# A two-layer graph network on Trainium2: edges in 2 MB loads, gathered rows apart from messages, degrees in PSUM, transposes and node stages a step ahead

## The chip, the cores and the metric

The kernel runs on one core of one Trainium2 chip. The metric is device time in microseconds (us) of that core, as a median of several executions; lower is better. A single execution was also taken by the hardware profiler, and all rows of the profile come from that one. Engines are named as in the profile: PE is TensorE (PEld its weight loads), DVE is VectorE, ACT is ScalarE, POOL is GpSimd and SP is SyncE, which only issues transfers here.

## The reference

There are N = 6250 nodes and E = 106250 edges, sorted by `dst`, with 256 float32 features each. `x` becomes `layernorm(x + L0(x))` and then `layernorm(x + L1(x))`; both layers use the same edges.

```python
# layer 0
msg = relu(x[src] + edge_attr)
agg = segment_sum(msg, dst, num_segments=N)
h = x + (x + agg)
f = bn1(h)
f = gelu(f @ W1.T + b1) @ W2.T + b2
L0 = bn2(h + f)
# layer 1
h = gelu((x[src] + edge_attr) @ W1m + b1m)
agg = segment_sum(h @ W2m + b2m, dst, num_segments=N)
deg = segment_sum(ones((E, 1)), dst, num_segments=N)
u = gelu((agg / maximum(deg, 1)) @ W1u + b1u) @ W2u + b2u
L1 = layernorm(x + u) * gamma + beta
```

## The kernel before, in words

**Work and tiles.** Edges are cut into tiles of 128 rows, and eight tiles make a span (`SPAN`, 1024 edges, V = 104 spans) of two groups of four (`GROUPS`, `G`). Nodes are cut into 25 blocks of 256 (`SB`). Because the edges are sorted, a span touches a short window of nodes, at most some 160. The sum over edges is done by matmuls with one-hot matrices in two stages: `into_slots` (L855) adds each tile's 128 rows into 32 slots, two tiles to the same 32, so a span ends as a 128 x 256 PSUM tile `slotP`; ACT copies it to `sums` (L861); `into_blocks` (L879) spreads the 128 slots over the nodes of their window, into the block's PSUM accumulator `acc`.

**What is done for a span.** POOL gathers the 128 source rows of each tile by an indirect transfer (L772), eight to a span, straight into a ring tile (`RING` = 5 tiles of 128 x 8 x 260). Edge features come in 0.5 MB loads of a group (`load_edges`, L760), three spans ahead (`AHEAD`). ACT lifts two edge tiles into PSUM (`lifted`, L809), DVE adds them to the gathered rows in the ring (`add_to_gathered`, L816), ACT applies Relu or Gelu to a group in place (`activated`, L824), DVE makes the one-hots (`one_hots`, L833; `slot_nodes`, L842; `hot3`, L873).

**Layer 1 uses linearity.** The nodes' part, `x1 @ W1m + b1m`, is computed once for each node at the end of layer 0 and stored as `proj` in DRAM, and this is what layer 1 gathers. The edges' part, `edge @ W1m`, needs transposed edge tiles: PE transposes a pair of tiles into PSUM (`turned`, L785, pool `eaP` with one buffer), ACT copies it to SBUF as `eaT` (L790), PE multiplies (`product`, L798, pool `workP` with four buffers). Half of this is done in layer 0 already: for the first group of every span the product `z` is stored to DRAM (`zst`) and loaded in place of edge features in layer 1; the second group's product is made in layer 1. `W2m` and `W1u` are multiplied into one matrix (`join_weights`) between the layers.

**Degrees.** Column 256 of each ring tile holds ones, so in layer 0 the slot sums also count edges. A one-row matmul for each part of a span (L886) spreads the counts over nodes, DVE adds them up (L890), and each block's degrees go to DRAM (`degd`) and come back in layer 1, broadcast to 128 partitions (`degb`).

**Order.** The program is scheduled by hand: each engine executes its instructions in the order in which the code issues them, and semaphores tie the engines together. `step_0(v)` (L1016) and `step_1(v)` (L1165) are one step each: gathers and, in layer 0, transposes of span v; adds, activations and one-hots of u = v - 1; slot and block sums of w = v - 2. On PE a step of layer 0 is: first transposes of v, slot sums of w, second transposes of v, first product of v, block sums of w, second product of v, and at the end node work. In layer 1 transposes and products are those of u. The node stages of a finished block (`nodes_0` L917 to L987, `nodes_1` L1080 to L1142) are generators; `advance()` runs one part of each at the end of every step. `normalized` (L891 on) is their layernorm, with a square root on ACT (L900).

Of the kernel before, what the change touches and what calls it, by code (L numbers as in the profile page):

```python
# [14 lines left out]
P = 128  # L15
D = 256
# [10 lines left out]
RING = 5  # L27
ROW = 260
AHEAD = 3
# [473 lines left out]
def kernel(  # L503
# [170 lines left out]
    degd = dram.tile([1, N], F32, name="degd")  # L674
    zst = dram.tile([len(window), P, G * D], F32, name="zst")
# [50 lines left out]
    GROUPS = SPAN // G  # L726

    with (
        tc.tile_pool(name="state", bufs=1) as state,
        tc.tile_pool(name="edges", bufs=(AHEAD + 1) * GROUPS) as ep,  # L730
# [4 lines left out]
        tc.tile_pool(name="eaP", bufs=1, space=bass.MemoryType.PSUM) as pse,  # L735
        tc.tile_pool(name="workP", bufs=4, space=bass.MemoryType.PSUM) as psw,
# [11 lines left out]

        ps = work()
# [5 lines left out]
        def load_edges(v, g):  # L755
            counts = tiles_of(v, g)
            ea = ep.tile([P, G, D], F32, name="ea")
            for j, k, n in runs(counts):
                r0 = (v * SPAN + g * G + j) * P
                nc.sync.dma_start(  # L760
                    out=ea[:n, j:k, :],
                    in_=edge_attr[r0 : r0 + (k - j - 1) * P + n, :].rearrange(
                        "(j p) d -> p j d", p=n
                    ),
                )
            return ea

        def gather(v, table):
            for g in range(GROUPS):
                for j, n in enumerate(tiles_of(v, g)):  # L770
                    t = v * SPAN + g * G + j
                    nc.gpsimd.indirect_dma_start(  # L772
                        out=rings[v % RING][:n, g * G + j, :D],
                        out_offset=None,
                        in_=table,
                        in_offset=bass.IndirectOffsetOnAxis(ap=src_sb[:n, t : t + 1], axis=0),
                    )

        def turned(v, g, q, ea):

            pair = tiles_of(v, g)[q : q + 2]
            pe = pse.tile([P, 2, KC, P], F32, name="eaP")
            for j, n in enumerate(pair):
                for k in range(KC):
                    nc.tensor.transpose(  # L785
                        pe[:, j, k, :n], ea[:n, q + j, k * P : (k + 1) * P], ident[:n, :n]
                    )
            eaT = hp.tile([P, 2, KC, P], F32, name="eaT", bufs=3)
            for j, k, n in runs(pair):
                nc.scalar.copy(eaT[:, j:k, :, :n], pe[:, j:k, :, :n])  # L790
            return pair, eaT

        def product(pair, eaT):

            ph = work()
            for j, n in enumerate(pair):
                for k in range(KC):
                    nc.tensor.matmul(  # L798
                        ph[:n, j, :], lhsT=eaT[:, j, k, :n], rhs=w1m_sb[:, k, :],
                        start=(k == 0), stop=(k == KC - 1),  # L800
                    )
            return ph

        def lifted(v, g, q, of):

            pair = tiles_of(v, g)[q : q + 2]
            ps = work()
            for j, k, n in runs(pair):
                nc.scalar.copy(ps[:n, j:k, :], of[:n, q + j : q + k, :])  # L809
            return ps  # L810

        def add_to_gathered(v, g, q, ps):
            at = g * G + q
            r = rings[v % RING]
            for j, k, n in runs(tiles_of(v, g)[q : q + 2]):
                nc.vector.tensor_add(  # L816
                    r[:n, at + j : at + k, :D], ps[:n, j:k, :], r[:n, at + j : at + k, :D]
                )

        def activated(v, g, func):  # L820
            r = rings[v % RING]
            for j, k, n in runs(tiles_of(v, g)):
                at = r[:n, g * G + j : g * G + k, :D]
                nc.scalar.activation(at, at, func)  # L824

        hots, hot2s, sums = {}, {}, {}

        def one_hots(v):

            hots[v] = hp.tile([P, SPAN, SLOTS], F32, name="hot")  # L830
            for j, n in enumerate(tiles_of(v, 0) + tiles_of(v, 1)):
                t = v * SPAN + j
                nc.vector.tensor_scalar(  # L833
                    hots[v][:n, j, :], ramp[:n, :SLOTS], slot[:n, t : t + 1], None,
                    op0=ALU.is_equal,
                )

        def slot_nodes(v):

            lo, hi = window[v]  # L840
            hot2s[v] = hp.tile([P, SB], F32, name="hot2")
            nc.vector.tensor_scalar(  # L842
                hot2s[v][:, : hi - lo], ramp[:, : hi - lo], float(lo), node_of[:, v : v + 1],
                op0=ALU.add, op1=ALU.is_equal,
            )

        def into_slots(v, width):

            counts = tiles_of(v, 0) + tiles_of(v, 1)
            hot, r = hots.pop(v), rings[v % RING]  # L850
            ps = pss.tile([P, D + 1], F32, name="slotP")
            for i in range(PAIR):
                for j in range(i, len(counts), PAIR):
                    n, q = counts[j], j // PAIR
                    nc.tensor.matmul(  # L855
                        ps[q * SLOTS : (q + 1) * SLOTS, :width],
                        lhsT=hot[:n, j, :], rhs=r[:n, j, :width],
                        start=(i == 0), stop=(i == PAIR - 1 or j + 1 == len(counts)),
                    )
            sums[v] = hp.tile([P, D + 1], F32, name="sums")  # L860
            nc.scalar.copy(sums[v][:, :width], ps[:, :width])  # L861

        def into_blocks(v, acc, opened, degs=None):

            its, hot, lo0 = sums.pop(v), hot2s.pop(v), window[v][0]
            for b, lo, hi in parts(v):
                at, fresh = hot[:, lo - lo0 : hi - lo0], b not in acc
                begins = opened(b) if fresh else False
                if begins:

                    lo, hi = b * SB, b * SB + shape(b)[0]
                    at = hp.tile([P, SB], F32, name="hot3")[:, : hi - lo]
                    nc.vector.tensor_scalar(  # L873
                        at, ramp[:, : hi - lo], float(lo), node_of[:, v : v + 1],
                        op0=ALU.add, op1=ALU.is_equal,
                    )
                cols = slice(lo - b * SB, hi - b * SB)
                for k in range(KC):
                    nc.tensor.matmul(  # L879
                        acc[b][:, k, cols], lhsT=its[:, k * P : (k + 1) * P], rhs=at,  # L880
                        start=(begins and k == 0),
                        stop=(last_span[b] == v and k == KC - 1),
                    )
                if degs is not None:
                    ps = work()
                    nc.tensor.matmul(  # L886
                        ps[:1, 0, : hi - lo], lhsT=its[:, D : D + 1], rhs=at,
                        start=True, stop=True,
                    )
                    nc.vector.tensor_add(degs[b][:, cols], degs[b][:, cols], ps[:1, 0, : hi - lo])  # L890
            return [b for b in sorted(acc) if last_span[b] == v]  # L891

        def normalized(tos, of, n, H):

            stats = npool.tile([P, SH, 6], F32, name="stats")
            mv = npool.tile([P, SH, 2], F32, name="mv")
            for h in range(H):
                nc.vector.bn_stats(stats[:n, h, :], of[:n, h, :])
                nc.vector.bn_aggr(mv[:n, h, :], stats[:n, h, :])  # L899
            nc.scalar.activation(mv[:n, :H, 1], mv[:n, :H, 1], AF.Sqrt, bias=eps[:n, :])  # L900
            nc.vector.reciprocal(mv[:n, :H, 1], mv[:n, :H, 1])
            if tos is None:
                return mv
            for h in range(H):
                nc.vector.tensor_scalar(
                    tos[:n, h, :], of[:n, h, :], mv[:n, h, 0:1], mv[:n, h, 1:2],
                    op0=ALU.subtract, op1=ALU.mult,
                )

        running = []  # L910

        def advance():

            for gen in list(running):
                if next(gen, "done") == "done":
                    running.remove(gen)


        def nodes_0(b, acc, xb, deg):
            width, H, n = shape(b)  # L920
# [94 lines left out]
        def step_0(v):  # L1015
            u, w = v - 1, v - 2  # L1016
            if v + AHEAD < V:
                load_0(v + AHEAD)
# [252 lines left out]
```

## Time and profile before

| what | value |
|---|---|
| median of 3 runs | 2815.48 us (2808.16 to 2825.01) |
| the profiled execution | 2831.86 us |
| its span | 2830.0 us |
| granted TensorE clock, mean of the span | 0.889 |
| PE busy | 2125.9 us, 75% |
| PE weight loads busy | 1607.0 us, 57% |
| POOL busy | 1575.0 us, 56% |
| DVE busy | 1430.2 us, 51% |
| ACT busy | 1348.9 us, 48% |
| moved by DMA | 531.79 MB, 188 GB/s on average |

A busy share is a mean over stretches that differ: start (0 to 99.5 us), layer 0 (to 1356.9), the seam between the layers (to 1461.9), layer 1 (to 2791.2) and the tail. A row of the profile names the line, the engine, the operation, what it writes and reads (out<-in with shapes), a count, the busy time with the mean of one, and the idle time of that engine just ahead of these instructions, with what ended it. PEclk is the share of full speed that PE was granted. "issue" as the cause of a wait means that the engine waited for nothing that the profile shows, and "remote" that the releaser isn't on record.

### The profile page before, as it was taken

How to read it: one execution, taken by the hardware profiler on the slowest of the kernel's cores; microseconds unless marked ns; L12 is line 12 of the kernel's file. 1: busy time of each engine (PE TensorE's matmuls, PEld its weight loads, DVE VectorE, ACT ScalarE, POOL GpSimd, SP SyncE). 2: the span in 40 equal slices, each digit the busy share in tenths (PEclk: the TensorE clock that was granted, in tenths of full speed). 3: DMA queues.
4: the chain of work that ended last, by engine and by line, in shares of the span. 5: the costliest groups of instructions: out<-in, count | busy, mean ns of one | idle time of the engine just before them, and what ended most of it. 6: DMA issues, size and time to landing. Idle time of an engine off the chain costs nothing.

```text
span 2830.0 us, 38426 instructions
## 1 busy us (share of the span) xinstructions
PE 2125.9 (75%) x11916; PEld 1607.0 (57%) x11916; DVE 1430.2 (51%) x4130; ACT 1348.9 (48%) x2143; POOL 1575.0 (56%) x1671
## 2 busy tenths in 40 slices
PE   2588888888888888888637777777777777777776
PEld 1465656665665666656425555655555556565554
DVE  3355555555555555556314554455455555454455
ACT  1355555555555555556313444454444444454454
POOL 4666566566566566564266555555556565565550
PEclk8799899899899999899868888988998898898988
DMA  6577677677777777675445555545555554555440
GB/s 197 177 233 222 224 229 224 221 230 227 224 226 220 231 230 232 220 226 177 152 129 178 165 171 181 164 159 182 172 165 183 166 181 156 168 185 169 160 152 11
DMA packets 313740, 531.79 MB, mean 188 GB/s; under 512 B 37989, under 2 KB 233144, under 8 KB 313400
## 3 DMA queue, kind: packets, MB, share of 16 engines
q1 hardware_dynamic: 231190, 307.82, 32.4%
q0 software_dynamic: 79744, 217.71, 26.1%
q10 hardware_dynamic: 2594, 3.71, 0.4%
q8 instruction: 100, 1.64, 0.2%
q14 instruction: 112, 0.92, 0.1%
HBM read 455.34 MB, written 73.75 MB: 187 GB/s over the span
## 4 chain that ended last, share of the span: by engine, by line
PE 50%; issue 18%; DVE 10%; POOL 7%; ACT 6%; another core or an unknown queue 5%; DMA 3%; POOLq 0%; DVEq 0%; SPq 0%; ACTq 0%
PE workP L798 22%; PE slotP L855 8%; POOL ring L772 7%; PE eaP L785 6%; PE acc L879 4%; DVE ring L816 2%; ACT eaT L790 2%; ACT ring L824 1%; PE workP L1125 1%; PE workP L1100 1%; PE workP L979 1%; DMA ring<-proj,src_sb 1%; PE workP L935 1%; PE workP L886 1%
## 5 line engine op out<-in xcount | busy, mean ns | idle before, releaser
L772 POOL DMA_INDIRECT ring<-proj,src_sb x831 | 787.5, 948 | 640.7 <-PE slotP L855 322.8
L772 POOL DMA_INDIRECT ring<-in_x_dram,src_sb x831 | 785.7, 945 | 531.8 <-PE slotP L855 239.0
L798 PE MATMUL workP<-w1m_sb,eaT 128*128 128x256 f32 x3324 | 944.6, 435 | 10.3 <-issue 6.6
L816 DVE TENSOR_TENSOR ring<-workP,ring 128x512 f32<-128x512 f32 x832 | 541.0, 683 | 668.9 <-PE workP L798 148.8
L824 ACT ACTIVATE ring<-ring 128x1024 f32<-128x1024 f32 x418 | 439.5, 1052 | 833.2 <-DVE ring L816 627.6
L798 PEld LDWEIGHTS workP<-w1m_sb,eaT 128*128 128x128 f32 x3324 | 707.5, 223 | 137.0 <-issue 24.8
L855 PE MATMUL slotP<-ring,hot 128*32 128x257 f32 (+1 forms) x3324 | 376.2, 409 | 270.4 <-ACT ring L824 164.1
L785 PE MATMUL eaP<-ident,ea 128*128 128x128 f32 x1662 | 299.1, 309 | 258.8 <-ACT eaT L790 184.6
L785 PEld LDWEIGHTS eaP<-ident,ea 128*128 128x128 f32 x1662 | 213.5, 155 | 386.7 <-ACT eaT L790 261.4
L855 PEld LDWEIGHTS slotP<-ring,hot 128*32 128x32 f32 x3324 | 139.6, 111 | 428.9 <-ACT ring L824 202.3
L790 ACT COPY eaT<-eaP 128x512 f32<-128x512 f32 x416 | 242.1, 582 | 228.4 <-PE slotP L855 119.3
L809 ACT COPY workP<-ea 128x512 f32<-128x512 f32 x624 | 344.9, 589 | 0.0
L879 PE MATMUL acc<-hot,sums 128*128 128x160 f32 (+19 forms) x1360 | 237.0, 303 | 101.5 <-DVE hot L873 62.1
L879 PEld LDWEIGHTS acc<-hot,sums 128*128 128x128 f32 x1360 | 216.5, 205 | 134.2 <-issue 92.1
L833 DVE TENSOR_SCALAR hot<-ramp,slot 128x32 f32<-128x32 f32 x1662 | 268.4, 256 | 0.0
L890 DVE TENSOR_TENSOR degs<-degs,workP 1x160 f32<-1x160 f32 (+24 forms) x170 | 40.3, 243 | 226.3 <-PE slotP L855 97.9
L1032 DVE COPY z<-workP 128x512 f32<-128x512 f32 x104 | 71.7, 689 | 153.6 <-PE workP L798 71.2
L1040 DVE COPY z<-workP 128x512 f32<-128x512 f32 x104 | 71.1, 684 | 148.7 <-PE slotP L855 90.9
L900 ACT ACTIVATE mv<-mv,eps 128x2 f32<-128x2 f32 (+1 forms) x75 | 22.2, 295 | 192.1 <-DVE mv L899 180.0
L1100 PE MATMUL workP<-fT,w 128*128 128x256 f32 (+1 forms) x400 | 94.7, 381 | 0.5 <-DVE fT L1090 0.5
L900 ACT ACT_TABLE_LOAD x73 | 93.7, 1283 | 1.3
L1125 PE MATMUL workP<-w2u_sb,uT 128*128 128x256 f32 (+1 forms) x392 | 89.0, 379 | 3.4 <-ACT uT L1109 3.4
(109 smaller groups left out, 1460.2 us busy)
## 6 DMA issues: line engine op xcount, KB each, us to landing
ea<-in_edge_attr_dram SPq DMA_DIRECT2D x310, 512.0 KB
zst<-z SPq DMA_DIRECT2D x104, 512.0 KB
ea<-zst SPq DMA_DIRECT2D x104, 512.0 KB
ring<-in_x_dram,src_sb POOLq DMA_INDIRECT x831
ring<-proj,src_sb POOLq DMA_INDIRECT x831
xb<-in_x_dram SPq DMA_DIRECT2D x24, 256.0 KB
x1d<-x SPq DMA_DIRECT2D x24, 256.0 KB
proj<-y SPq DMA_DIRECT2D x24, 256.0 KB
```

Of the source, the lines that this page charges most:

```text
L772: nc.gpsimd.indirect_dma_start(out=rings[v % RING][:n, g * G + j, :D], out_offset=None, in_=table, in_offset=bass.IndirectOffsetOnAxis(ap= ...
L785: nc.tensor.transpose(pe[:, j, k, :n], ea[:n, q + j, k * P : (k + 1) * P], ident[:n, :n])
L790: nc.scalar.copy(eaT[:, j:k, :, :n], pe[:, j:k, :, :n])
L798: nc.tensor.matmul(ph[:n, j, :], lhsT=eaT[:, j, k, :n], rhs=w1m_sb[:, k, :], start=(k == 0), stop=(k == KC - 1),)
L809: nc.scalar.copy(ps[:n, j:k, :], of[:n, q + j : q + k, :])
L816: nc.vector.tensor_add(r[:n, at + j : at + k, :D], ps[:n, j:k, :], r[:n, at + j : at + k, :D])
L824: nc.scalar.activation(at, at, func)
L833: nc.vector.tensor_scalar(hots[v][:n, j, :], ramp[:n, :SLOTS], slot[:n, t : t + 1], None, op0=ALU.is_equal,)
L855: nc.tensor.matmul(ps[q * SLOTS : (q + 1) * SLOTS, :width], lhsT=hot[:n, j, :], rhs=r[:n, j, :width], start=(i == 0), stop=(i == PAIR - 1 ...
L879: nc.tensor.matmul(acc[b][:, k, cols], lhsT=its[:, k * P : (k + 1) * P], rhs=at, start=(begins and k == 0), stop=(last_span[b] == v and k ...
L1100: nc.tensor.matmul(ps[:, o - i, :width], lhsT=w12[:, k, o * P : (o + 1) * P], rhs=mT[:, k, :width], start=(k == 0), stop=(k == KC - 1),)
L1125: nc.tensor.matmul(ps[:n, h, :], lhsT=uT[:, k, h * P : h * P + n], rhs=w2u_sb[:, k, :], start=(k == 0), stop=(k == UC - 1),)
```

## The change

- **Edge loads**: one tile holds the edges of two spans. In layer 0 it is filled by one load of 2 MB, in layer 1 by one 1 MB load of `z` and two 0.5 MB loads of edges. `z` is stored once for two spans, 1 MB. `AHEAD` = 2 counts pairs of spans.
- **Gathered rows**: gathers write a pool `gathered` of three tiles, 128 x 8 x 256. The DVE add reads lifted edges (or products) and gathered rows, and writes the ring, which has three tiles now. Slot sums therefore depend on no gather directly.
- **PSUM**: pools `eaP` (1) and `workP` (4) become `liftA` (1), `liftB` (1) and `workP` (3). Lifts use the first two; transposes, products and node stages share the third.
- **Degrees** are counted in layer 1: ACT copies the count column of `slotP` broadcast to 128 x 128 (`counts`), and one matmul for each part adds it into a PSUM tile that stays open through the layer (`deg`, the buffer of `liftB`), so the degrees are on all partitions. L886, L890, `degd` and `degb` are gone.
- **Order**: transposes of span v are made in step v, in both layers, and their products in step v + 1. On PE a step is: slot sums of w, first product of u, first transposes of v, block sums of w, second product of u, second transposes of v, node products. `slot_nodes` and `hot3` are made a step earlier. Within the slot sums the tiles go in reverse order.
- **Node stages**: each block has a list of stages, one a step, of three parts: `early` (ahead of the step's first product), `late` (behind the second group's activation) and `products` (PE, at the end). A node product's result is therefore used in the next step. Layer 0 has six stages, layer 1 seven.
- **`join_weights`** is called ahead of the first step, not between the layers.

```diff
-RING = 5
+RING = 3
-AHEAD = 3
+AHEAD = 2
...
-        tc.tile_pool(name="edges", bufs=(AHEAD + 1) * GROUPS) as ep,
+        tc.tile_pool(name="edges", bufs=AHEAD + 1) as ep,
+        tc.tile_pool(name="gathered", bufs=3) as gp,
...
-        tc.tile_pool(name="eaP", bufs=1, space=bass.MemoryType.PSUM) as pse,
-        tc.tile_pool(name="workP", bufs=4, space=bass.MemoryType.PSUM) as psw,
+        tc.tile_pool(name="liftA", bufs=1, space=bass.MemoryType.PSUM) as pla,
+        tc.tile_pool(name="liftB", bufs=1, space=bass.MemoryType.PSUM) as plb,
+        tc.tile_pool(name="workP", bufs=3, space=bass.MemoryType.PSUM) as psw,
...
             for j, k, n in runs(counts):
-                r0 = (v * SPAN + g * G + j) * P
+                r0 = (i * BOTH + j) * P
                 nc.sync.dma_start(
-                    out=ea[:n, j:k, :],
+                    out=eas[i][:n, j:k, :],
...
                     nc.gpsimd.indirect_dma_start(
-                        out=rings[v % RING][:n, g * G + j, :D],
+                    out=gathered[v][:n, j, :],
...
                 nc.vector.tensor_add(
-                    r[:n, at + j : at + k, :D], ps[:n, j:k, :], r[:n, at + j : at + k, :D]
+                    rings[v % RING][:n, at + j : at + k, :D], ps[:n, j:k, :],
+                    gathered[v][:n, at + j : at + k, :],
                 )
...
+        def slots_kept(v, width):
+            ps = slots.pop(v)
+            sums[v] = hp.tile([P, D + 1], F32, name="sums")
             nc.scalar.copy(sums[v][:, :width], ps[:, :width])
+            if width > D:
+                counts[v] = hp.tile([P, P], F32, name="counts")
+                nc.scalar.copy(counts[v], ps[:, D : D + 1].to_broadcast([P, P]))
...
+                    nc.tensor.matmul(
+                        deg[:, b % 2, lo - b * SB : hi - b * SB], lhsT=counts[v],
+                        rhs=hot[:, lo - lo0 : hi - lo0], start=False, stop=(last_span[b] == v),
+                        skip_group_check=True,
+                    )
...
-                    nc.tensor.matmul(
-                        ps[:1, 0, : hi - lo], lhsT=its[:, D : D + 1], rhs=at,
-                        start=True, stop=True,
-                    )
-                    nc.vector.tensor_add(degs[b][:, cols], degs[b][:, cols], ps[:1, 0, : hi - lo])
...
+            return [
+                [opened, None, first],
+                [gelu, None, second],
+                [added, measured, None],
+                [normal, None, turn],
+                [keep, None, third],
+                [projected, None, None],
+            ]
```

The new step of layer 0 (gathers and slot sums come first, as named above):

```python
            early()
            if adds:
                ph = product(*eaTs.pop((u, 0)))
            if comes:
                slots_kept(w, D)
            if adds:
                nc.vector.tensor_copy(zs[u // 2][:, u % 2, 0:2, :], ph)
            if goes:
                first = turned(pair_of(v, 0, 0), edges_0(v, 0, 0))
            if adds:
                qs = range(0, len(tiles_of(u, 1)), 2)
                lifts = {q: lifted(pair_of(u, 1, q), edges_0(u, 1, q), q // 2) for q in qs}
                for q in qs:
                    add_to_gathered(u, 1, q, lifts[q])
            full = into_blocks(w, acc, opened_0) if comes else []
            if goes:
                eaTs[v, 0] = kept(*first)
            if adds:
                activated(u, 0, AF.Relu)
                ph = product(*eaTs.pop((u, 2)))
            if goes:
                first = turned(pair_of(v, 0, 2), edges_0(v, 0, 2))
...
            late()
            if adds:
                slot_nodes(u, False)
            products()
```

## The prediction

> **What bounds the kernel now.** I read the page's totals first, then cut the span into five stretches at the starts of `slotP` (L855), then took each engine's waits in the two long stretches, then the rows by shape, then the timeline at the seam of the layers. The stretches (start:end, length, busy us of PE, PEld, DVE, ACT, POOL, granted clock, DMA share, GB/s):
>
> ```profile
> 0.00:99.50 99.50, 26.72 (x110) 20.14 (x110) 28.57 (x90) 13.94 (x22) 45.21 (x55) 0.78 0.57 178
> 99.50:1356.90 1257.40, 1041.79 (x6078) 773.56 (x6076) 683.30 (x1973) 674.26 (x1103) 742.34 (x786) 0.92 0.70 222
> 1356.90:1461.90 105.00, 39.30 (x179) 27.93 (x178) 17.39 (x50) 19.65 (x31) 45.42 (x48) 0.67 0.42 132
> 1461.90:2791.20 1329.30, 1001.79 (x5479) 773.55 (x5478) 679.79 (x1961) 628.16 (x965) 742.04 (x783) 0.89 0.52 166
> 2791.20:2830.00 38.80, 16.26 (x74) 11.87 (x74) 21.20 (x60) 12.94 (x23) 0.00 (x0) 0.74 0.06 19
> ```
>
> The second and fourth stretch are layers 0 and 1, 102 steps each: 12.33 and 13.03 us a step. PE is busy 10.21 and 9.82 us of it and idle 2.11 and 3.21. The first, third and last stretch are start, seam and tail. PE's waits, layer 0, then layer 1 (us in total, times, longest):
>
> ```profile
> PE slotP L855 <- issue: 69.6, 117, 1.7
> PE eaP L785 <- ACT eaT L790: 65.2, 56, 3.1
> PE eaP L785 <- ACT mv L900: 31.5, 10, 3.4
> PE eaP L785 <- issue: 27.7, 18, 4.4
> ```
> ```profile
> PE slotP L855 <- ACT ring L824: 150.3, 65, 5.9
> PE eaP L785 <- ACT eaT L790: 90.1, 54, 3.3
> PE acc L879 <- issue: 31.7, 18, 3.5
> PE acc L879 <- DVE hot L873: 17.4, 10, 1.8
> PE slotP L855 <- DMA ring<-proj,src_sb: 13.4, 9, 2.0
> ```
>
> So PE is first, with two kinds of bubble: transposes that wait until ACT has copied the one `eaP` buffer, and slot sums that wait for eight gathers' semaphores (layer 0) or for the Gelu of the step before (layer 1). POOL is close behind: its gather takes 0.945 us and the next starts 0.30 us later when nothing holds it, 1.25 us, eight to a span, so no step can be under 10.0 us. Now POOL waits for PE, because a gather writes a ring tile that `slotP` must have read:
>
> ```profile
> L772 POOL DMA_INDIRECT ring<-in_x_dram,src_sb x831 | 785.7, 945 | 531.8 <-PE slotP L855 239.0
> L798 PE MATMUL workP<-w1m_sb,eaT 128*128 128x256 f32 x3324 | 944.6, 435 | 10.3 <-issue 6.6
> L890 DVE TENSOR_TENSOR degs<-degs,workP 1x160 f32<-1x160 f32 (+24 forms) x170 | 40.3, 243 | 226.3 <-PE slotP L855 97.9
> ```
>
> DMA is not it: 222 GB/s in layer 0, while stretches of 5 us in the same trace reach 360. DVE and ACT are near half busy.
>
> At the seam POOL runs 40 gathers (five ring tiles) ahead from about 1387 to 1451 us, and in that time the others see PE's results late. ACT's and DVE's rows of the timeline (start, length, line, in brackets the idle time before):
>
> ```profile
> 1420.58 0.37 ACT L861 COPY sums<-slotP 128x256 f32<-128x256 f32 x1 [14.15 <-remote]
> 1431.14 0.59 ACT L790 COPY eaT<-eaP 128x512 f32<-128x512 f32 x1 [10.19 <-remote]
> 1453.51 0.69 DVE L816 TENSOR_TENSOR ring<-workP,ring 128x512 f32<-128x512 f32 x1 [44.59 <-remote]
> ```
>
> PE had ended that `slotP` at 1407.0 by its own row. The start has the same picture: slot sums at 60.2, the next at 99.5.
>
> **Layer 0, part by part.** From 12.33 us a step:
> - Transposes run a step ahead, in rotating work buffers, and their copies come later in ACT's queue. The three `eaP` rows go: 124.4 us of 1257.4.
> - Slot sums wait on one semaphore instead of eight gather queues, since the gathers now end in tiles of their own that only the DVE add reads: the `slotP <- issue` row goes, 69.6. The wait for the gather's landing moves to the DVE add; behind it on DVE stand the one-hots and z copies, and DVE is 54% busy.
> - Degrees leave layer 0: 336 one-row matmuls, 57.0 us of PE, with 170 adds of 243 ns on DVE (hidden now, nothing for them).
> - The clock. Eight products in a full-clock burst take 1.99 us, 249 ns each, so 1616 would take 402 us; the row has 457. By the rule of the Trainium skill ("TensorE: Matmul & The Clock Gate", Why this matters for your kernels: no idle gap of PE over about 3 us, or one idle window puts it back to half clock) filling the bubbles would return all 55. The stretch has a granted clock of 0.92 though its longest waits are 3 to 4 us and rare, so the clock drops there without such gaps too. I take half, 28.
> - 2 MB edge loads: 310 issues of 0.5 MB become some 52 in layer 0, and z goes out 1 MB a time. SP waits for none of PE's work and DMA has room: nothing. Bounds: a gather's packets queuing behind a bigger burst cost up to 0.3 us a step; fewer issues gain nothing visible.
>
> PE's sum: 1257.4 - 124.4 - 69.6 - 57.0 - 28 = 978, 9.6 us a step: under POOL's 10.0. So the bound passes to POOL, plus its own remote waits (26.8 us in layer 0, 0.26 a step): 10.3. The two are then 0.7 us apart with just three gathered tiles between them, and PE's load is uneven (a node product of 1.6 to 3.6 us falls in three of 4.17 steps). Coupling costs between 0 and 1.0 us (half of the 194 us of waits back); I take 0.5: **10.8 us, 102 x 1.53 = 156 us gained**.
>
> Here a second rule speaks against the change: "Perfetto Trace Analysis", Optimization Strategy, says that a bubble that keeps repeating can mean too few buffers, and this change cuts `workP` from 4 to 3 while transposes move into it, and rings from 5 to 3. By the rule the wait `eaP <- ACT eaT` would come back under the name `workP`. By the trace a work buffer is held for about 2 us plus a 0.58 us copy, and 3 buffers serve 4 edge tiles plus one node tile a step: 5 x 2.6 = 13 us of the 30 that three offer. I follow the trace, unless results are seen late.
>
> **Layer 1.** From 13.03:
> - Transposes ahead: 90.1 + 10.5 go. `hot3` is made a step early: 17.4. Gather landing no longer on PE: 13.4 + 8.3 (`slotP <- issue`). Half of the `acc <- issue` row, as no row names its cause: 16. Sum 156.
> - Degrees come in: one matmul for a part beside L879's two, in the same shape. L879 is 117.8 us here, so +59 on PE; a broadcast copy of 128x128 on ACT (near the 0.37 us of L861, under PE's blocks) and a memset on DVE a block: nothing. It also drops the degree broadcast loads.
> - The row `slotP <- ACT ring L824`, 150.3, stays. In both versions the second product of the span ends, then DVE adds (0.69), ACT takes the Gelu (1.06), and the next step begins with slot sums; PE has only four transposes (0.6) and the node products to lay beside it. 1.5 us a step. For the clock I count nothing therefore.
>
> Net 97 less 2 for ACT's longer queue: **95, to 12.1 us a step**. PE's own work is then 8.8 to 10.1 us and POOL's 10.0; what is late next is that Gelu.
>
> **Start, seam, tail.** With three gathered tiles POOL can run only 24 gathers ahead (30 us, not 50), so late results last less long: seam 105 to about 70 (35). `join_weights` leaves the seam for the start, about +10, against 18 of its 39 us stall: 8 gained. The node stages are 7 steps for 5, so the tail grows by 5.
>
> Sum: 156 + 95 + 35 + 8 - 5 = 289. The profiled execution took 2831.86 (span 2830.0), 16.4 above the median of 2815.48. 2832 - 289 = 2543; minus 16 for the median: **2526**.
>
> **Rivals.**
> - A, the above, 0.55. Own range 2440 to 2620 (coupling 0 to 1.0 in layer 0, 0.4 either way in layer 1).
> - B, POOL is the only bound in both layers, because the node stages fill the Gelu's shadow: 10.3 and 10.6 a step. 102 x (2.03 + 2.43) + 38 = 493: 2322. For it: 10.0 is a floor that POOL reaches at the seam, and its row is waits on PE. Against: the Gelu chain is not touched. 0.17.
> - C, the bubbles come back in other places (three work buffers, PE's results seen late), and only start and seam gain: 2815 - 38 = 2777. For it: ACT and DVE rows that read `remote` or `issue` mean late results, and no edit removes those. 0.21; of this 0.03 ends within 0.5%, which is about what a measurement of this kernel can tell from no change.
> - D, slower: ACT's queue. The copy of the slot sums, which PE's block matmuls need, now stands behind `early()`: a node Gelu with its table load (1.28 us) and two activations (0.45 each), itself waiting for PE's node product. PE covers slot sums, a product, transposes: 1.08 + 1.99 + 0.60 = 3.7 us. Gelu steps alone are 1 to 2 in 4.17, 2.2 us, inside the cover. If PE's result is seen 4 us late in each step, the copy comes 4.1 + 1.4 - 3.7 = 1.8 us late over all of A: 204 x 1.8 = 367, 2526 + 367 = 2893. It decides from 289 / 204 = 1.4 us a step. Only stretches with gathers running free show such lateness at length. 0.07.
>
> That the change doesn't do what it says I exclude: in the built order PE's transposes stand a step ahead of their products, and slot sums hold one wait.
>
> **How the numbers follow.** Faster by over 0.5%: A, B and most of C, 0.90; same 0.03; slower D, 0.07. The range goes from B's 2322, less 12, to 2760, which leaves out D and the upper part of C.
>
> **What would show it.** Right: no PE wait of transposes on ACT above 20 us a layer, no `slotP <- issue`; POOL's wait names a DVE add and its share rises from 56% to over 60%; layer 0 between 10.3 and 11.3 us a step; `slotP <- ACT ring` still over 100 us in layer 1. Wrong: a PE wait `workP <- ACT` or `acc <- ACT sums` of over 100 us (C, D); DMA over 260 GB/s with POOL idle.

## The result, and the profile after

The changed kernel took 2987.2 us (median of 4 runs, 2974.5 to 3003.2) against 2820.2 us of the kernel before beside it: a ratio of 1.060 (1.0535 to 1.0669), slower, where 2526 us had been forecast. The profiled execution has a span of 2972.7 us, 142.7 more than before.

The same five stretches, cut at the same starts of slot sums (now L899), of which the second to fourth are shown (columns as before: start:end, length, busy us of PE, PEld, DVE, ACT, POOL, granted clock, DMA share, GB/s):

```profile
70.05:1505.80 1435.75, 1034.39 (x5755) 789.59 (x5754) 644.37 (x1782) 670.05 (x1103) 757.92 (x799) 0.83 0.62 195
1505.80:1580.80 75.00, 33.56 (x166) 24.50 (x170) 17.80 (x50) 18.53 (x34) 31.32 (x33) 0.75 0.59 196
1580.80:2930.10 1349.30, 1028.98 (x5813) 792.14 (x5815) 692.97 (x1978) 685.52 (x1131) 757.16 (x798) 0.87 0.50 162
```

| stretch | before, us | after, us | moved | forecast |
|---|---|---|---|---|
| start | 99.5 | 70.0 | -29.5 | -8 |
| layer 0, 102 steps | 1257.4 (12.33 a step) | 1435.8 (14.08) | +178.4 | -156 |
| seam | 105.0 | 75.0 | -30.0 | -35 |
| layer 1, 102 steps | 1329.3 (13.03) | 1349.3 (13.23) | +20.0 | -95 |
| tail | 38.8 | 42.6 | +3.8 | +5 |

So the loss lies in layer 0. Start, seam and tail together went as said or better (-55.7 us, where -38 had been forecast). Now the waits of layer 0: PE's three longest and one that was to go, POOL's longest, and ACT's two longest (us in total, times, longest).

```profile
PE acc L935 <- ACT sums L910: 157.0, 57, 4.8
PE workP L1003 <- ACT eaT L820: 51.5, 5, 11.5
PE acc L935 <- issue: 35.9, 19, 3.6
PE slotP L899 <- issue: 30.7, 35, 3.4
```
```profile
POOL gathered L800 <- DVE ring L847: 434.9, 85, 13.8
```
```profile
ACT sums L910 <- remote: 233.0, 46, 8.5
ACT eaT L820 <- remote: 226.2, 41, 13.3
```

Of the four rows that the change was to remove from PE, the three of the transposes went (what transposes wait for copies is 8.9 us now). The fourth, slot sums on "issue", fell from 69.6 to 30.7 us and did not go. In their place PE's block sums wait for the copy of the slot sums, and ACT, which makes that copy, reads "remote": by PE's own record the slot sums end 4.1 us before their copy starts, and ACT is idle for 3.0 us of this. POOL waits 434.9 us for DVE's adds; before it waited 239.0 for slot sums. A piece of ACT's timeline in layer 0 (start, length, line, idle time before it), and the last matmul on PE ahead of its second row:

```profile
135.56 2.00 ACT L856 ACTIVATE ring<-ring 128x1024 f32<-128x1024 f32 x2
149.96 0.59 PE L828 MATMUL workP<-w1m_sb,eaT 128*128 128x256 f32 x1 [0.63 <-issue]
151.51 0.59 ACT L820 COPY eaT<-workP 128x512 f32<-128x512 f32 x1 [13.95 <-PE workP L828]
```

ACT stands still for 13.95 us. In that time POOL issues the gathers of two spans in one go, 16 of them from 128.6 to about 148. There are about 12 such joined bursts in layer 0 after the change (11 to 13, by how short a pause between two gathers counts as none) and none before. Gaps of over 6 us in which neither ACT nor DVE is at work add up to 156 us in layer 0 (16 gaps), and to nothing before. Not all of this is a result seen late: in the piece shown PE itself goes slowly, its product of eight matmuls (1.99 us in a full-clock burst) running from 140.75 to 150.55 with "issue" between the single matmuls. In 5 of the 16 gaps PE starts nothing; in the other 11 it is at work for 2.9 to 6.3 us. Why it goes slowly in this one is not shown.

### The profile page after: what moved, and what is told of

It is laid out like the page before. It is cut to its first block, busy times and chain, and to the rows that moved or that the text cites. A ratio compares the mean times of both kernels' runs of the same rounds, so it can differ in the third digit from the quotient of the medians.

```text
span 2972.7 us, 34773 instructions
## 1 busy us (share of the span) xinstructions
PE 2139.7 (72%) x11916; PEld 1636.1 (55%) x11916; DVE 1405.4 (47%) x3960; ACT 1401.9 (47%) x2315; POOL 1579.1 (53%) x1671
## 4 chain that ended last, share of the span: by engine, by line
PE 38%; another core or an unknown queue 18%; ACT 14%; issue 11%; DVE 10%; DMA 5%; POOL 3%; ACTq 0%; DVEq 0%; POOLq 0%
PE workP L828 16%; PE acc L935 5%; PE workP L812 4%; PE slotP L899 4%; DVE ring L847 4%; POOL gathered L800 3%; ACT ring L856 3%; ACT eaT L820 3%; DMA gathered<-proj,src_sb 2%; PE workP L1240 2%; ACT liftA L841 2%; DMA gathered<-in_x_dram,src_sb 2%; PE liftB L920 2%; PE workP L1003 2%
## 5 line engine op out<-in xcount | busy, mean ns | idle before, releaser
L800 POOL DMA_INDIRECT gathered<-in_x_dram,src_sb x831 | 788.8, 949 | 692.5 <-DVE ring L847 460.3
L800 POOL DMA_INDIRECT gathered<-proj,src_sb x831 | 788.5, 949 | 628.0 <-DVE ring L847 355.5
L820 ACT COPY eaT<-workP 128x512 f32<-128x512 f32 x416 | 240.6, 579 | 566.5 <-remote 275.0
L899 PE MATMUL slotP<-ring,hot 128*32 128x256 f32 (+1 forms) x3324 | 292.6, 444 | 211.6 <-DVE hot L865 109.2
L847 DVE TENSOR_TENSOR ring<-liftA,gathered 128x512 f32<-128x512 f32 x416 | 286.7, 689 | 285.7 <-ACT liftA L841 113.7
L847 DVE TENSOR_TENSOR ring<-workP,gathered 128x512 f32<-128x512 f32 x208 | 143.1, 688 | 438.3 <-remote 172.3
L812 PE MATMUL workP<-ident,ea 128*128 128x128 f32 x1662 | 269.1, 288 | 82.8 <-DVE ring L847 37.7
L812 PEld LDWEIGHTS workP<-ident,ea 128*128 128x128 f32 x1662 | 221.4, 151 | 151.5 <-DVE ring L847 47.4
L841 ACT COPY liftA<-ea 128x512 f32<-128x512 f32 x416 | 246.9, 594 | 100.3 <-DVE ring L847 52.4
L899 PEld LDWEIGHTS slotP<-ring,hot 128*32 128x32 f32 x3324 | 107.0, 120 | 335.4 <-ACT ring L856 174.1
L920 PE MATMUL liftB<-hot,counts 128*128 128x160 f32 (+24 forms) x340 | 66.1, 310 | 125.2 <-ACT counts L913 39.9
L847 DVE TENSOR_TENSOR ring<-liftB,gathered 128x512 f32<-128x512 f32 x208 | 141.3, 680 | 0.0
```

What stands on the lines that cost most here:

```text
L800: nc.gpsimd.indirect_dma_start(out=gathered[v][:n, j, :], out_offset=None, in_=table, in_offset=bass.IndirectOffsetOnAxis(ap=src_sb[:n, t ...
L812: nc.tensor.transpose(pe[:, j, k, :n], of[:n, j, k * P : (k + 1) * P], ident[:n, :n])
L841: nc.scalar.copy(ps[:n, j:k, :], of[:n, j:k, :])
L847: nc.vector.tensor_add(rings[v % RING][:n, at + j : at + k, :D], ps[:n, j:k, :], gathered[v][:n, at + j : at + k, :],)
L899: nc.tensor.matmul(ps[q * SLOTS : (q + 1) * SLOTS, :width], lhsT=hot[:n, j, :], rhs=r[:n, j, :width], start=q not in seen, stop=(i == 0),)
L920: nc.tensor.matmul(deg[:, b % 2, lo - b * SB : hi - b * SB], lhsT=counts[v], rhs=hot[:, lo - lo0 : hi - lo0], start=False, stop=(last_span ...
```

## What the traces say about late results

I had seen at the seam that results come late while POOL gathers, and had taken it for a matter of long free runs. It goes on in ordinary steps too. For each PE instruction that updates PE's semaphore (the counter by which other engines learn of a result) I took the time from the end of its record to the next recorded update, in layer 0 of the kernel before: 0.4 us on average while POOL is not gathering, 0.2 in the first two us of a burst of eight gathers, 1.4 at 2 to 4 us, 2.7 at 6 to 8 us. (7% of PE's updates are missing from the record, so these means are somewhat high.) Over the 148 bursts of eight in the whole execution, PE's updates come at 0.01 to 0.2 a us between 8 and 11 us after a burst's start, and at 6.3 a us in the twelfth, some 1.5 us behind the burst's last gather. DVE's and ACT's updates, of which a third is missing, thin out too.

So a step is a burst of 10 us, a release of what was held up some 1.5 us behind it, and then whatever POOL still needs before it may start again. Before, POOL needs the slot sums, which are among the results released: the gap from one burst to the next is 2.7 us on average in layer 0. After, it needs the last DVE add, and behind the released results there still stand lifts, a copy of z and two to four adds: the gap is 4.9 us, and the next burst begins 0.27 us behind an add. The sum closes: 9.7 + 2.7 = 12.4 us before, where 12.33 was measured; after, a single burst and its gap take 9.7 + 4.1 = 13.8 us, and a joined one takes 30.3 us for two spans, together 14.2 a step, where 14.08 was measured. That is theory L, in which the move of the gathers' release from PE's slot sums to DVE's add costs the time. Rival Q puts the loss down to ACT's order and to three work buffers instead of four (D and C of the prediction). Rival T puts it down to the 2 MB loads.

## The experiments

Ratios are to the kernel before in the same series of runs. The kernel before took 2812, 2782, 2219, 2215 and 2217 us in the five series; the big step between the second and the third matters and comes up below.

**e1: the ring apart, alone, in the kernel before.**
```diff
-RING = 5
+RING = 3
+        tc.tile_pool(name="gathered", bufs=3) as gp,
...
-                        out=rings[v % RING][:n, g * G + j, :D],
+                        out=gathered[v][:n, g * G + j, :],
```


> The kernel before, with one part of the change alone: gathers write a pool of three tiles of their own and three ring tiles are left, so that a gather is released by the last DVE add of the span three back and no longer by PE's slot sums. Theory L (results of all engines are seen late while POOL issues gathers, and the change moved POOL's bursts onto the slot sums' way through ACT to the block sums): slower, 2880 to 2980 us, layer 0 over 13 us a step. Rival Q (the loss is in ACT's order and in three work buffers instead of four, which this kernel does not have): 2770 to 2830 us, as the kernel before or a little less.

3028 us, ratio 1.076 (1.0724 to 1.0788), above the range of L: this one part costs more than the whole change. Layer 0 and POOL's wait in it:

```profile
63.87:1583.35 1519.48, 1131.88 (x6079) 834.67 (x6080) 692.12 (x1975) 675.16 (x1103) 755.84 (x800) 0.81 0.60 185
```
```profile
POOL gathered L776 <- DVE hot L837: 520.9, 99, 9.9
```

14.90 us a step in layer 0 (9.7 of burst and 5.2 of gap, where the gap was 2.7). POOL waits 520.9 us for DVE (the row names the one-hots that stand behind the last add; each burst begins 0.27 us behind that add). Nothing of ACT's order or PSUM was touched. Q falls as the main cause. In layer 1 the same part costs nothing: 12.96 us a step against 13.03 before. POOL's wait there, before and in e1, changes its name and not its size:

```profile
POOL ring L772 <- PE slotP L855: 322.8, 141, 11.5
POOL gathered L776 <- DVE ring L820: 302.7, 88, 10.8
```

So a release by the add is not dear in itself. Theory L says why it is in layer 0; why it is free in layer 1 no run shows.

**e5: the same part undone, in the changed kernel.**
```diff
-RING = 3
+RING = 5
-        tc.tile_pool(name="gathered", bufs=3) as gp,
...
-                    out=gathered[v][:n, j, :],
+                    out=rings[v % RING][:n, j, :D],
```


> The changed kernel with one part undone: gathers write the ring tiles again (five of them) and there is no gathered pool, so PE's slot sums release a gather, as before the change. All else is the changed kernel: 2 MB loads, degrees in PSUM, the order a step ahead, three work buffers. Theory L (what counts is how deep in POOL's burst the slot sums end): they end near the burst's start again, layer 0 goes from 14.1 to about 12.3 us a step, 2770 to 2840 us. Rival Q (ACT's order and three work buffers): 2950 to 3020 us.

2795 us, ratio 1.0037 (1.001 to 1.0064), where the changed kernel has 1.060. The rows of both layers:

```profile
102.60:1356.50 1253.90, 973.15 (x5755) 766.85 (x5758) 645.89 (x1782) 667.63 (x1103) 745.09 (x786) 0.88 0.69 222
1452.60:2747.10 1294.50, 992.09 (x5813) 780.02 (x5816) 682.21 (x1979) 679.57 (x1131) 743.09 (x783) 0.90 0.51 167
```

12.29 and 12.69 us a step. With e1 that shows from both sides that the gathers' own tiles are the loss. Both edits change two things at once, though: what releases a gather's tile, and how many tiles there are (five for gathers before, three after). More than three gathered tiles were not tried, so the share of each is not shown. And the time was foretold for a wrong reason, so the hit is luck in part. I had expected the slot sums to end early in a burst again. They end some 7 us into it, and their copy starts 4.1 us behind them, as after the change. What went back is the gap between bursts, 4.9 to 2.8 us, and POOL's wait:

```profile
POOL ring L798 <- ACT sums L908: 219.6, 79, 10.2
```

It names ACT's copy of the slot sums, not the slot sums themselves: here bursts begin 0.3 us behind that copy, which still comes ahead of the step's last adds. So the late copy alone is not the price; by these figures POOL's restart is.

**e2: POOL made to wait for the copy of the slot sums.**
```diff
+                if goes:
+                    nc.gpsimd.tensor_copy(paced, sums[w][:, :1])
+            if goes:
+                gather(v, x)
```


> The changed kernel, where POOL waits before a span's eight gathers until ACT has copied the slot sums of the same step (a one-column copy on POOL reads that tile), and the gathers are called behind it. Theory L: the way from slot sums to block sums no longer lies under a burst; 11.5 to 12.3 us a step in both layers, 2500 to 2700 us. Rival Q: a further wait on a kernel bound elsewhere, 2980 to 3100 us.

2897.5 us, ratio 1.033 (1.0288 to 1.0363): by the ratios 2.6% better than the change, and far from the 2500 to 2700 expected. Layer 0 went to 13.03 us a step and layer 1 to 13.67. The burst still covers the next slot sums (they end about 7 us into it). A burst of 10 us in a step of 12 leaves little room to put it where nothing is in flight.

**e7: 0.5 MB loads in the changed kernel.** The load of layer 0 is cut into four.
```diff
+                for a in range(j, k, G):
+                    e = min(k, a + G)
...
-                    out=eas[i][:n, j:k, :],
+                        out=eas[i][:n, a:e, :],
```


> The changed kernel with the 2 MB edge loads of layer 0 cut into 0.5 MB loads, in the same tile and at the same place. Theory L: 2960 to 3010 us, no change. Rival T (big loads stand in the gathers' way and stretch the bursts): layer 0 gains a microsecond a step or more, 2850 to 2900 us.

2960.5 us, ratio 1.060 (1.0532 to 1.0668) in its series, the same as the change. T falls: the size of layer 0's edge loads neither helps nor harms here.

**e6 and e8: ACT's and DVE's order.** The copy of the slot sums goes ahead of the node stages' early part, and the one-hots go behind the first adds; e8 does this with e5's ring.
```diff
+            if comes:
+                slots_kept(w, D)
             early()
...
-                one_hots(u)
                 activated(u, 1, AF.Relu)
```


> The changed kernel with the copy of the slot sums ahead of the node stages' early part in ACT's queue, and the eight one-hots made on DVE behind the first adds instead of behind the last; gathers stay apart. Theory L: the lateness in layer 0 stays, layer 1 gains what stood in ACT's and DVE's queue, 2900 to 2970 us. Rival Q: the loss is this order, 2750 to 2850 us.

> Both edits, the ring as the gathers' target and the earlier copy and one-hots. Theory L: the gain of the ring in layer 0 and that of the order in layer 1 add up, 2690 to 2780 us, under both kernels. Rival Q: no further gain over the edit of the order alone.

e6: 2928.5 us, ratio 1.049 (1.0423 to 1.056), in L's range. It is a per cent better than the change, with intervals that overlap. e8: 2847 us, 1.021 (1.0155 to 1.0257), worse than e5 by 1.7%; L and Q both missed that. In e8 layer 1 took 13.32 us a step against e5's 12.69, with 13 to 20 joined bursts against 3 to 6 (by how short a pause counts as none). That the two go together is all that is shown.

**e3 and e4: no gathers on POOL.** Both kernels read other rows than the reference asks for, by plain transfers of the same size.
```diff
-                nc.gpsimd.indirect_dma_start(
...
+                r0 = t * 47 % (N - P)
+                nc.sync.dma_start(out=gathered[v][:n, j, :], in_=table[r0 : r0 + n, :])
```


> The changed kernel with each gather replaced by a plain transfer of 128 neighbouring rows of the same table, issued from SP: the rows are other ones than the reference asks for, the bytes are the same, and POOL issues nothing. Theory L: the late results go, PE's waits fall below 15%, 2300 to 2500 us. Rival Q, and a rival in which the transfers themselves are what is late: 2850 to 3000 us.

> The kernel before with the same plain transfers in place of gathers (other rows, same bytes). Theory L: also faster, 2450 to 2700 us, and by less than the changed kernel gains by the same edit, as its own bursts lay better. Rival Q: 2750 to 2830 us.

The changed kernel takes 2269 us (ratio 0.807), the kernel before 2188 us (0.778), in the series in which the latter took 2812. Both lie below the ranges that L gave. So 22% of the time goes when the gathers leave POOL, though the same bytes move faster (291 and 281 GB/s in layer 0, where the gathering kernels had 195 and 222). The edit changes the issuing engine, the kind of queue and the rows (neighbouring ones) together; which of these counts it can't tell. Layer 0 takes 9.43 us a step after and 9.89 before. The degrees that left it had 57.0 us of PE, 0.56 a step, so no gain of the new order shows there. Layer 1 takes 11.33 after and 10.03 before: a second loss, which the first trace hardly shows (13.23 against 13.03). PE's longest waits in layer 1 of the changed kernel without gathers:

```profile
PE liftB L916 <- ACT counts L909: 111.4, 40, 4.4
PE slotP L895 <- DVE hot L861: 53.1, 33, 1.6
PE liftB L916 <- DVE liftB L1358: 34.3, 12, 4.7
```

The first matmul of the block sums is now that of the degrees, and it waits for ACT's broadcast copy of the counts, behind lifts and the node Gelu with its table load.

**e12: that order mended, still without gathers.** It is e6 with e3's transfers.

> Two edits together in the changed kernel: plain transfers from SP of other rows in place of gathers (as before), and the slot sums' copy ahead of the node stages' early part with the one-hots behind the first adds. Without POOL's bursts the changed kernel lost 1.3 us a step in layer 1 against the one before. If that is the copy and one-hots standing late in ACT's and DVE's queue, layer 1 goes from 11.4 to 10.2 to 10.7 us a step and the time to 2140 to 2210 us; if it is the degrees' matmuls and stages on PE, 2240 to 2280 us.

2185 us: layer 1 from 11.33 to 10.44 us a step, 90 us, in the expected range. The wait for counts fell from 111.4 to 23.3 us. So two thirds of the second loss is the order on ACT and DVE (the two edits were not tried apart, and e3 ran in another series).

**e9, e10, e11: pauses on POOL.** Small memsets ahead of each burst in the changed kernel (e9), in the middle of each burst (e10) or after every second gather (e11) in the kernel before.
```diff
+            for _ in range(6):
+                nc.gpsimd.memset(pause, 0.0)
```


> The changed kernel, with six small memsets on POOL (1.5 to 2 us together) ahead of each span's eight gathers, so that two spans' bursts can't join into one of 16. Theory L (in layer 0 of the changed kernel 24 spans' gathers came in 12 joined bursts, and ACT and DVE stood still together for 156 us in gaps of over 6 us): those gaps fall below 40 us, layer 0 goes from 14.1 to 12.6 to 13.2 us a step, 2820 to 2900 us. Rival W (the joined bursts are a sign, not the cause; the pause only lengthens POOL's work): 2980 us or more.

> The kernel before, with four small memsets on POOL (about 1.2 us) between the fourth and the fifth gather of each span. Theory L1 (results held up in a burst get through in any gap of a microsecond): they come 2 to 4 us earlier, steps of 11.3 to 12.0 us, 2650 to 2780 us. Rival F (what was held up comes 1 to 1.5 us after POOL's last gather, whatever lies between): a step is burst and flush, 1.2 us more, 2900 to 3050 us.

> The kernel before, with two small memsets on POOL (about 0.6 us) after every second gather of a span, three such gaps. Theory L1: as with one gap, or better, 2650 to 2780 us. Rival F: 1.8 us of POOL's time more in a step, 2950 to 3100 us.

Ratios 1.21, 1.144 and 1.227. But in this series the kernel before took 2219 us, not 2800, so there was nothing for a pause to mend. The steps came to POOL's own sum. In the timelines six memsets in a row take 2.17 us and four 1.46, and the next gather starts 0.1 us later than it would behind a gather: 10.0 + 2.17 + 0.1 = 12.3 for e9 (12.32 in both layers), 10.0 + 1.46 + 0.1 = 11.6 for e10 (11.64 and 11.55). They say that POOL's time is then the bound, and nothing on theory L.

**e13 to e18: the same again, twice.**

> The changed kernel unaltered, beside the kernel before, on whichever chip comes. If the kernel before takes about 2800 us (a chip that shows late results under POOL's bursts): ratio 1.05 to 1.07. If it takes about 2220 us (a chip like the third): without lateness the ratio is that of the plain transfers, 1.02 to 1.06 by theory L, as layer 1 loses in ACT's and DVE's queue what layer 0 gains.

> The changed kernel with six memsets (1.9 us by the profile of the third chip) ahead of each span's gathers. On a chip with late results: theory L, the joined bursts and the standstills over 6 us go, ratio to the kernel before 1.00 to 1.04; rival W, 1.06 or more. On a chip like the third: 1.20 to 1.22 as there.

> The kernel before with four memsets (1.3 us by the profile of the third chip) between the fourth and fifth gather. On a chip with late results: theory L1 (what is held up gets through in a gap), ratio 0.94 to 0.99; rival F (it comes only after POOL's last gather), 1.04 to 1.09. On a chip like the third: 1.14 as there.

> The kernel before unaltered, for its trace on whichever chip comes. On a chip like the third (no late results): by theory L POOL's own 10.0 us a step is the bound in both layers, 10.0 to 10.4 us a step in layer 0 and 10.0 to 10.6 in layer 1, against 9.95 and 11.55 of the changed kernel on such a chip. On a chip with late results: 12.4 and 13.2, as in its first trace.

> The changed kernel with six memsets (1.9 us) ahead of each span's gathers. On a chip with late results: theory L, joined bursts and standstills over 6 us go, ratio to the kernel before 1.00 to 1.04; rival W, 1.06 or more. On a chip without: 1.21 as twice before.

> The kernel before with four memsets (1.3 us) between the fourth and fifth gather. On a chip with late results: theory L1 (held-up results pass in a gap), ratio 0.94 to 0.99; rival F (only after POOL's last gather), 1.04 to 1.09. On a chip without: 1.14 as twice before.

Both series came to the same condition: before 2215 and 2217 us; e14 and e17 1.211 and 1.209, e15 and e18 1.145 and 1.143. The changed kernel (e13) took 2346 us, ratio 1.0595 (1.0571 to 1.0619). So it loses 6% here too, and in the other layer. Both layers of the kernel before (e16), then of the changed kernel (e13):

```profile
61.40:1080.60 1019.20, 916.83 (x6079) 712.97 (x6081) 693.73 (x1980) 672.46 (x1104) 766.62 (x811) 0.98 0.88 277
1145.30:2173.00 1027.70, 851.43 (x5479) 676.84 (x5477) 682.12 (x1961) 628.91 (x965) 765.16 (x807) 1.00 0.69 218
```
```profile
67.90:1073.50 1005.60, 870.14 (x5754) 697.94 (x5752) 635.62 (x1781) 670.91 (x1102) 758.11 (x801) 0.94 0.87 278
1129.40:2301.80 1172.40, 956.42 (x5810) 760.54 (x5810) 689.56 (x1979) 676.82 (x1131) 765.91 (x809) 0.92 0.59 187
```

Layer 0 takes 9.99 us a step before and 9.86 after, layer 1 10.08 and 11.49. In e16 POOL's row reads as follows:

```profile
L772 POOL DMA_INDIRECT ring<-in_x_dram,src_sb x831 | 786.4, 946 | 286.0 <-issue 132.6 <-DMA ring<-in_x_dram,src_sb 37.2 <-DVE astray L751 33.1
```

POOL waits for no slot sums; it runs without a stop at 1.25 us a gather, and from PE's record to its update there is 0.01 us. The loss of 145 us in layer 1 is 105 of busy PE and 40 of idle PE. Of the busy part 65 are the degrees' matmuls (L920); the products grew from 390.2 to 445.0 and the block sums from 112.9 to 134.2 at a clock of 0.92 instead of 1.00; the slot sums lost 21. PE's waits there are those of e3: 110.1 us for counts, 46.3 for one-hots, 34.5 for the memset of the degrees.

## Why the prediction was wrong, by its own steps

- **"Slot sums wait on one semaphore ... since the gathers now end in tiles of their own."** The row fell to 30.7 us. But an edit that moves where gathers land also moves what releases their buffer, and here it left three of these instead of five. I costed the landing and not when POOL may start again. This is the step that failed. The gathers' own three tiles are worth +260 us in layer 0 when put in alone (e1), and with them undone all but 0.4% of the change's 6% is gone (e5), in the condition of the prediction. How much of it is the release and how much the number of tiles is open.
- **"So the bound passes to POOL ... 10.3 ... Coupling costs between 0 and 1.0 us."** This is the term in which that step shows. The sum took PE and POOL for two engines that meet on average. With late results they run in turn: burst 10 us, release, gap. I had written the cause under C (`remote` rows "mean late results, and no edit removes those") but took it for a thing of long free runs, and gave it no sum for each step. The coupling term stood at 0.5 us and measured 14.08 - 10.3 = 3.8. In the later condition it measured nothing: 9.86 us a step, which is POOL's floor.
- **The terms of PE in layer 0.** Most of the waits that were to go went, and so did the degrees; others came in their place (157.0 us for the copy of the slot sums). Without gathers it all gave 0.46 us a step (9.89 to 9.43), less than the degrees alone. Without gathers those waits are smaller to begin with: 55.8 us for the transposes' copies in e4's layer 0.
- **"A broadcast copy ... (under PE's blocks) ... nothing."** Wrong by its place. The copy is ahead of PE's blocks, since the degrees' matmul is the first of them. It and the one-hots behind the last add cost 111.4 + 53.1 us of waits in e3, and about 90 us of time (e12).
- **"+59 on PE" for the degrees** was near: 65.0 in e13, 66.1 on the changed kernel's page.
- **"`slotP <- ACT ring L824`, 150.3, stays."** It fell to 21.8 us in layer 1, while the one-hots took 101.9 of its place. The chain of add and Gelu alone does not make 150.3: in e16, without late results, the row is 31.7 us.
- **Rival D** had the right sign and a number 94 us short, 2893, with results seen about 4 us late in each step. The copy does start 4.1 us behind the slot sums in layer 0. But its mechanism, the node stages' early part in ACT's queue, was worth about a per cent (e6), and e5 has the same lateness with no loss. I gave it 0.07.
- **The two rules.** POOL's 85 waits in layer 0 are a repeated bubble, and the rule of the Trainium skill that such bubbles can mean too few buffers ("Perfetto Trace Analysis", Optimization Strategy), which I set aside, would have named three work buffers, or three tiles for gathers instead of five. The runs speak against the first: e5 has three work buffers and no loss, e1 has four and the whole loss. The second they leave open, as said at e5. PE's clock in layer 0 was 0.83 with PE waits of up to 11.5 us, and 0.98 in e16, whose waits there end at 2.8 us. That agrees in direction with the rule of "TensorE: Matmul & The Clock Gate" (Why this matters for your kernels); no run here varies the gaps alone. I had expected the clock to rise by half of what was missing; it fell.
- **Two readings** of the page were off, with little weight in the sums. "310 issues of 0.5 MB" are those of both layers, 103 of which remain. At the seam the gathers run from 1391.5 us, and there are 48 up to 1451, not 40 from 1387.

**What stays open.** Whether the number of the gathers' tiles or what releases them makes the loss, and why the same edit is free in layer 1. Which part of the gathers makes results late: e3 and e4 change engine, queue and rows at once. Whether joined bursts cause the standstills of 156 us, or only go with them: e9 was to tell, and all three tries came to the other condition. They are no large part of the loss, though. In the changed kernel's layer 0 a joined burst and its gap take 30.3 us for two spans, two single ones 27.6, which makes some 30 us of the 178; e1 loses more with a single joined burst, and e6 has twice as many and takes 13.92 us a step. It is open too whether a gap within a burst lets results through (e10, e11). And no run shows what sets the condition. The record numbers the chips of the experiments' series 5, 13, 3, 6 and 5; number 5 stands for 2812 us and for 2217 us, so the number alone doesn't. No version tried that gathers the right rows beats the kernel before in either condition; e5 comes within 0.4%.

## What to carry to other kernels

When a transfer gets a new target, ask not only who waits for its landing but what releases its buffer, how late in the step that is, and how many buffers there are now; price it on the queue that waits for it. When engines seem to wait for "remote" or "issue" in a trace, find out with what it goes together (here, with the place in POOL's burst) before making any sum from average busy times. And a short copy that feeds the first matmul of a group is priced by its place in its engine's queue (here 111.4 us of waits), not by its length.

## What the runs showed of the hardware

- While POOL issues indirect gathers (0.95 us each, 0.30 between), results of PE, ACT and DVE can reach the other engines late, many of them some 1.5 us behind the burst's last gather; for PE 0.4 us outside bursts, 2.7 us late in one. Plain transfers from SP in place of the gathers took 22% off the kernel before in that condition (2812 to 2188 us).
- It is not always so. On other occasions the same kernel with gathers of the same duration ran in 2217 us with updates 0.01 us behind the records. A change can thus lose by the same ratio in both conditions (1.060 and 1.0595) in two different layers, and a prediction made from one trace holds for its condition only.
- A memset of 128x256 on POOL took 0.32 us, six in a row 2.17 us, and with them POOL's sum alone set the step (e9: 12.32 us in both layers).
